# Six VectorE exps per head group instead of five, with the square of their polynomial on GpSimd

## The chip, the cores and the metric

The kernel runs on one core of one Trainium2 chip. A core has TensorE (matrix products, written PE in the profile, its weight loads PEld), VectorE (DVE), ScalarE (ACT), GpSimd (POOL) and SyncE (SP), which here only issues transfers (DMAs). Each engine works through its own queue in order and waits on semaphores for the others. The metric is the device time of one execution in microseconds (us): 11,025.7 us is the median of three runs of the kernel before (11,016.71 to 11,026.11).

## The reference, cut to what matters

The program is a graph network of four layers on 3,327 nodes with 128 features. Nearly all of its time goes to layer 0, an attention with 128 heads of 8 features, in which the adjacency matrix is added to the scores twice:

```python
q = (x @ Wq.T).reshape(d, n, h)          # d = 128 heads, n = 3327, h = 8
k = (x @ Wk.T).reshape(d, n, h)
v = (x @ Wv.T).reshape(d, n, h)
a = jnp.einsum('dnh,dmh->dnm', q, k) * scale
a = a + spatial_encoding + edge_encoding  # both are adj
a = jax.nn.softmax(a, axis=2)
out = jnp.einsum('dnm,dmh->dnh', a, v)
...
return out @ Wo.T
```

So for each of 128 heads a 3,327 x 3,327 matrix of exps is needed. All is fp32.

## The kernel before, in words

**Tiling.** The queries are cut into 7 chunks `c` of 476 columns (`CW`; the last has 472), the heads into 32 groups `g` of four heads `j`, the keys into 13 pairs `q` of two tiles of 128 keys, called even (r = 0) and odd (r = 1). A unit `u` is one (c, g, q): a pair of key tiles for four heads; there are 7 x 32 x 13 = 2,912. A head group is 13 units; there are 224.

**One unit.** PSUM has seven banks `S` for scores and one, `po`, for the sums of values. VectorE seeds a bank with adj minus a bound (`seed`, L641). TensorE adds the scores of head 0, ScalarE takes exp of twice the bank (`exps`, L662 for both banks of a unit in one wide instruction, L665 for one bank where the unit's banks are the first and last of S, which happens to one unit in seven). For heads 1 to 3 TensorE does not start afresh: it adds the scores of head j and subtracts those of head j - 1 in one product (`scores`, L650), as the q tile `QS` holds minus the q of head j - 1 beside the q of head j, and `KT` both heads' keys. The exps of head j of unit u are at slot 4u + 3j of a list of slots `i`, so neighbouring units are interleaved; the seeds, scores and value products (`values`, L705, four heads beside one another) are put between them by the loop over `i` at the end of the function. The order on each engine is the order of the program.

**Exps by hand.** In the units whose q is in `BY_HAND`, the exp of head 0 and the odd tile is made by VectorE: the bank then holds the plain score without seed, VectorE copies it out scaled (L683), seeds the bank for head 1 right behind it, and multiplies up a polynomial of the score in three steps (L687); a last one (L689) multiplies with `EA`, the bare exp of the seed, which is made once per chunk and pair by VectorE (L674) and ScalarE (L675) in `bare`. These steps are a generator, `hand_exp`, of which the slots draw one or two steps at a time. As they end late, `heads_of` lets the value products of the next unit go first. The tile e0 that the result goes into has five buffers.

**Loads.** For the next group `loads` calls, at pair 1, `load_qk`: for each head four transfers of keys into `KT` (16 partitions of 6,656 bytes each, or twice that for heads 1 and 2, where they go to two places) and six or nine small ones of q into `QS` and `QZ`; then one of v. SP issues them; both KT and QS have two buffers by group. At pair 4 GpSimd negates the q of heads 0 to 2 into the place of the next head (`negate_q`, L566, six instructions of 32 partitions), spreads v (L576) and makes a small copy (`all_here`, L580) for which the next group's first score waits. A transfer uses one of eight semaphores in turn, and SP waits for the one before on the same semaphore.

**Other work in the loop.** At the end of a group VectorE copies `po` out (L713) and GpSimd issues four stores (L717), 2.5 pairs into the next group. In about half of the groups 128 rows of adj are partly loaded, turned by VectorE (L288) and searched for row maxima (L292) for a later chunk (class `Square`).

Of the kernel before, what the change touches and what calls it, by code (L numbers as in the profile page):

```python
# [10 lines left out]
F32 = mybir.dt.float32  # L11
# [6 lines left out]
ALU = mybir.AluOpType  # L18
# [70 lines left out]
def gnn_kernel(ctx: ExitStack, tc: tile.TileContext, x, adj, Wq, Wk, Wv, Wo, embed, layer,  # L89
# [435 lines left out]
    with tc.tile_pool(name="e1", bufs=1) as e1, tc.tile_pool(name="e_adj", bufs=28) as e_adj, \  # L525
# [15 lines left out]
        def load_qk(c, g):  # L541

            b = (c * NG + g) % 2
            w, c0 = width_of(c), c * CW
            for j in range(4):
                d = 4 * g + j
                k0, nk = max(0, j - 1), 1 if j in (0, 3) else 2
                q_d = qS_d[:, :, d * N + c0:d * N + c0 + w].rearrange("i e n -> (i e) n")
                for r in range(2):
# [5 lines left out]
                    for q_s in [QS[b][:, j, :]] + [QZ[b]] * ((r, j) == (1, 1)):  # L555
                        nc.sync.dma_start(q_s[r0:r0 + 16, :w].bitcast(F32), q_d)
                        for i in range(2):
                            nc.sync.dma_start(q_s[r0 + 16 + 8 * i:r0 + 24 + 8 * i, :w].bitcast(F32),
                                              q_d[8 - 8 * i:16 - 8 * i])

        def negate_q(c, g):
            b, w = (c * NG + g) % 2, width_of(c)
            for j in range(3):
                for r in range(2):
                    r0 = 64 * r + 32 * (1 - j % 2)
                    nc.gpsimd.tensor_scalar(QS[b][r0:r0 + 32, j + 1, :w], QS[b][r0:r0 + 32, j, :w].bitcast(F32),  # L566
                                            -1.0, 0.0, op0=ALU.mult, op1=ALU.add)
# [27 lines left out]
        with tc.If(loose < 1), tc.manual_schedule():  # L595
# [74 lines left out]

            def bare(c, q):

                w = width_of(c)
                nc.vector.tensor_tensor(EA[q][:, :w], adj_of[c][2 * q + 1][:, :w], shift_of[c][:, :w], op=ALU.subtract)  # L674
                nc.scalar.activation(EA[q][:, :w], EA[q][:, :w], AF.Exp, scale=2.0)  # L675

            def hand_exp(u):
# [11 lines left out]
                nc.vector.scalar_tensor_tensor(e, e, EXP_C[0], EA[pairs[u][2]][:, :w], op0=ALU.add, op1=ALU.mult)  # L689

            def heads_of(u, r):


                first = (u, r)
                if by_hand(u) and r == 1:
                    first = (u + 1, 0)
                elif by_hand(u - 1):
                    first = (u, 1) if r == 0 else (u - 1, 1)
                return [first] + [(u, r)] * 3

            def values(u, r):
                c, g, q = pairs[u]
                w, k = width_of(c), c * NG + g
                for j, (v, of) in enumerate(heads_of(u, r)):
                    nc.tensor.matmul(po[32 * j:32 * j + H + 1, :w], VA[k % 2][:, 2 * pairs[v][2] + of, j, :],  # L705
                                     e_of[v, j][:, 1 - of, :w], start=(q == 0 and r == 0),
                                     stop=(q == NQ - 1 and r == 1))
# [11 lines left out]
            def loads(u):  # L719
# [40 lines left out]
            load_qk(0, 0)  # L760
            shift_of[0] = load_shift(0)
            negate_q(0, 0)
# [728 lines left out]
```

## Time and profile before

| what | value |
|---|---|
| median of the runs | 11,025.7 us |
| the profiled execution, its own time | 11,023.3 us |
| its span, first to last instruction | 11,021.5 us |
| mean granted TensorE clock | 0.985 |
| VectorE's seeds, L641 | 5,824 of 689 ns |
| VectorE's steps, L683, L687, L689 | 5,600 of 650 to 733 ns |
| GpSimd's negations, L566 | 1,344 of 819 ns |
| GpSimd's stores, L717 | 896 of 532 ns |
| transfers into KT | 1,792 of 208 KB and 1,792 of 104 KB |
| transfers into QS and QZ | 6,048 of 15 or 30 KB |

The page gives busy times; an engine's instruction counts as busy from when its waits are over, also while the instruction before it is still running, so that durations can be longer than the pace at which results come. The pace is seen in the timeline, from start to start. "Idle before" is the time in which an engine had nothing under way, with what ended it.

### The profile page before, as it was taken

How to read it: one execution, taken by the hardware profiler on the slowest of the kernel's cores; microseconds unless marked ns; L12 is line 12 of the kernel's file. 1: busy time of each engine (PE TensorE's matmuls, PEld its weight loads, DVE VectorE, ACT ScalarE, POOL GpSimd, SP SyncE). 2: the span in 40 equal slices, each digit the busy share in tenths (PEclk: the TensorE clock that was granted, in tenths of full speed). 3: DMA queues.
4: the chain of work that ended last, by engine and by line, in shares of the span. 5: the costliest groups of instructions: out<-in, count | busy, mean ns of one | idle time of the engine just before them, and what ended most of it. 6: DMA issues, size and time to landing. Idle time of an engine off the chain costs nothing. (4 is left out here: it accounts for less than half of the span.)

```text
span 11021.5 us, 206200 instructions
## 1 busy us (share of the span) xinstructions
PE 10563.2 (96%) x72876; PEld 3424.9 (31%) x72876; DVE 8675.8 (79%) x13503; ACT 10046.2 (91%) x13789; POOL 2177.6 (20%) x3149
## 2 busy tenths in 40 slices
PE   4599999999999999999999999999999999999889
PEld 2123322332223323233332232323323332333544
DVE  5588887888878888788887888878888778887655
ACT  3599999999999999999999999999999999999330
POOL 5122121121112121112122121112112112121101
PEclk7799999999999999999999999999999999999999
DMA  8755555555555554555556555565545545454678
GB/s 248 252 99 96 94 98 108 94 98 96 94 111 98 92 98 85 105 98 98 89 95 119 91 97 91 95 116 97 91 88 97 99 89 88 81 87 72 201 234 281
DMA packets 695348, 1257.08 MB, mean 114 GB/s; under 512 B 195218, under 2 KB 555049, under 8 KB 691244
## 3 DMA queue, kind: packets, MB, share of 16 engines
q1 hardware_dynamic: 644044, 1114.42, 51.0%
q0 software_dynamic: 50272, 129.37, 4.2%
q8 instruction: 590, 9.67, 0.4%
q14 instruction: 442, 3.62, 0.2%
HBM read 1096.53 MB, written 146.60 MB: 113 GB/s over the span
## 5 line engine op out<-in xcount | busy, mean ns | idle before, releaser
L662 ACT ACTIVATE e<-S 128x952 f32<-128x952 f32 (+1 forms) x9024 | 8307.7, 1073 | 40.9 <-PE S L650 27.5
L705 PE MATMUL po<-e,VA 128*9 128x476 f32 (+1 forms) x46592 | 5738.7, 564 | 32.3 <-DVE OS L713 13.0
L641 DVE TENSOR_TENSOR S<-a,shb 128x476 f32<-128x476 f32 (+1 forms) x5824 | 4011.0, 689 | 1337.4 <-ACT e L662 974.5
L650 PE MATMUL S<-QS,KT 64*128 64x476 f32 (+1 forms) x22176 | 4546.8, 444 | 90.2 <-DVE S L641 49.8
L650 PEld LDWEIGHTS S<-QS,KT 64*128 64x128 f32 x22176 | 2083.3, 184 | 5100.3 <-issue 1289.3
L665 ACT ACTIVATE e<-S 128x476 f32<-128x476 f32 (+1 forms) x4128 | 2411.0, 685 | 3.4 <-PE S L650 2.5
L687 DVE SCALAR_TENSOR_TENSOR e<-e,h 128x476 f32<-128x476 f32 (+1 forms) x2240 | 1547.6, 691 | 77.0
L566 POOL TENSOR_SCALAR QS<-QS 32x476 fp32r<-32x476 f32 (+1 forms) x1344 | 1100.3, 819 | 1578.9 <-DMA QS<-qS_d 984.3
L717 POOL DMA_DIRECT2D oT_d<-OS x896 | 472.2, 532 | 4477.1 <-DVE OS L713 4432.9
L705 PEld LDWEIGHTS po<-e,VA 128*9 128x9 f32 x46592 | 691.0, 88 | 1639.8 <-issue 1521.3
L683 DVE TENSOR_SCALAR h<-S 128x476 f32<-128x476 f32 (+1 forms) x1120 | 727.8, 650 | 261.6 <-PE S L650 260.0
L689 DVE SCALAR_TENSOR_TENSOR e<-e,EA 128x476 f32<-128x476 f32 (+1 forms) x1120 | 821.2, 733 | 0.0
L687 DVE SCALAR_TENSOR_TENSOR e<-h 128x476 f32<-128x476 f32 (+1 forms) x1120 | 767.3, 685 | 0.0
L1091 PE MATMUL pu<-strip,y 128*128 128x512 f32 (+2 forms) x1456 | 599.8, 566 | 31.0 <-DVE y L952 14.8
L650 PE MATMUL S<-QZ,KT 64*128 64x476 f32 (+1 forms) x1120 | 487.2, 435 | 11.8 <-DVE S L641 8.1
L576 POOL COPY VA<-VR 128x832 f32<-128x832 f32 x224 | 243.1, 1085 | 985.3 <-DMA VR<-v_d 743.2
L1091 PEld LDWEIGHTS pu<-strip,y 128*128 128x128 f32 (+1 forms) x1456 | 271.6, 191 | 304.7 <-issue 271.9
L1095 DVE TENSOR_REDUCE deg<-strip 128x1 f32<-128x1536 f32 (+1 forms) x104 | 193.8, 1881 | 58.6 <-DMA strip<-adjT 41.9
L650 PEld LDWEIGHTS S<-QZ,KT 64*128 64x128 f32 x1120 | 205.3, 183 | 108.4 <-DVE S L641 60.3
L288 DVE STREAM_TRANSPOSE cols<-rows 128x416 f32<-128x416 f32 x208 | 205.0, 990 | 27.0 <-DMA rows<-in_adj_dram 18.9
L713 DVE COPY OS<-po 128x476 f32<-128x476 f32 (+1 forms) x224 | 146.2, 653 | 97.9 <-PE po L705 97.9
L1044 ACT COPY uT<-pu 128x512 f32<-128x512 f32 (+1 forms) x21 | 11.1, 554 | 222.7 <-PE pu L1091 222.7
(255 smaller groups left out, 1975.8 us busy)
## 6 DMA issues: line engine op xcount, KB each, us to landing
KT<-kS_d SPq DMA_DIRECT2D x1792, 208.0 KB
KT<-kS_d SPq DMA_DIRECT2D x1792, 104.0 KB
VR<-v_d SPq DMA_DIRECT2D x224, 416.0 KB
QS<-qS_d SPq DMA_DIRECT2D x3072, 14.9 KB
QS<-qS_d SPq DMA_DIRECT2D x1536, 29.8 KB
adjT<-cols SPq DMA_DIRECT2D x26, 1664.0 KB
a<-adjT SPq DMA_DIRECT2D x156, 238.0 KB
strip<-adjT POOLq DMA_DIRECT2D x39, 895.5 KB, 5.2
```

The lines of the kernel that those rows point to most:

```text
L566: nc.gpsimd.tensor_scalar(QS[b][r0:r0 + 32, j + 1, :w], QS[b][r0:r0 + 32, j, :w].bitcast(F32), -1.0, 0.0, op0=ALU.mult, op1=ALU.add)
L576: nc.gpsimd.tensor_copy(VA[(c * NG + g) % 2][:, :, :, 0:H], v.rearrange("p j (t e) -> p t j e", e=H))
L641: touch(u, [r], nc.vector.tensor_tensor(bank(u, r), adj_of[c][2 * q + r][:, :w], shift_of[c][:, :w], op=ALU.subtract))
L650: x = nc.tensor.matmul(bank(u, r), KT[b][64 * r:64 * r + 64, max(0, j - 1), q * P:(q + 1) * P], q_s[64 * r:64 * r + 64, :w], start=hand an ...
L662: touch(u, (0, 1), nc.scalar.activation(e[:, :, :w], S[:, odd:even + 1, :w], AF.Exp, scale=2.0))
L665: touch(u, [r], nc.scalar.activation(e[:, 1 - r, :w], bank(u, r), AF.Exp, scale=2.0))
L683: touch(u, [1], nc.vector.tensor_scalar(s, bank(u, 1), EXP_ARG, None, op0=ALU.mult))
L687: nc.vector.scalar_tensor_tensor(e, s if k == 3 else e, EXP_C[k], s, op0=ALU.add, op1=ALU.mult)
L689: nc.vector.scalar_tensor_tensor(e, e, EXP_C[0], EA[pairs[u][2]][:, :w], op0=ALU.add, op1=ALU.mult)
L705: nc.tensor.matmul(po[32 * j:32 * j + H + 1, :w], VA[k % 2][:, 2 * pairs[v][2] + of, j, :], e_of[v, j][:, 1 - of, :w], start=(q == 0 and r ...
L717: nc.gpsimd.dma_start(oT_d[:, d * N + c * CW:d * N + c * CW + w], o[32 * j:32 * j + H + 1, :w])
L1091: nc.tensor.matmul(ps[:, :k], y[:m, t, :], s[:m, c * 4 * P - c0:c * 4 * P - c0 + k], start=(t == 0), stop=(t == NT - 1))
```

## The change

The units with an exp by hand are now at pairs 0, 2, 4, 6, 8 and 10, six per group. The polynomial is rewritten as a product of two quadratics that share one square, plus a constant: VectorE adds a constant to the score (z), GpSimd squares z into e, and VectorE makes three more steps of it, each with two tensors as inputs: four VectorE instructions in place of five. The leading coefficient moves into EA as a shift of its argument. The seed of the bank is still behind the first step. `heads_of` is taken out, and e0 has four buffers. In a chunk's preparation the shift of EA (VectorE) and its exp (ScalarE) are a pair apart.

The loads of the next group are split: at pair 1 all keys, then the q of head 0, then v. At pairs 3, 5 and 7 GpSimd negates one head over all 128 partitions into the next head's place, and SP then loads that head's q over a part of it. The spreading of v and the small copy are at pair 8. On GpSimd's queue each group now has: the square of pair 0, that of pair 2, the four stores, the negation of head 0, the square of pair 4, the negation of head 1, the square of pair 6, the negation of head 2, the square of pair 8, the copies, the square of pair 10.

```diff
-EXP_C = (0.9999990463256836, 2.2162604331970215, 2.4563632011413574, 1.8291265964508057)
-EXP_ARG = 0.9023826718330383
-BY_HAND = (0, 2, 5, 7, 10)
+EXP_C = (0.25674915313720703, 0.05050157010555267, 1.8002841472625732, 0.8117094039916992)
+EXP_LEAD = -0.2054332047700882
+BY_HAND = (0, 2, 4, 6, 8, 10)
...
-        def load_qk(c, g):
+        def load_k(c, g):
...
+        def load_q(c, g, j):
+            b = (c * NG + g) % 2
+            w, c0, d = width_of(c), c * CW, 4 * g + j
+            q_d = qS_d[:, :, d * N + c0:d * N + c0 + w].rearrange("i e n -> (i e) n")
+            for r in range(2):
+                r0 = 64 * r + 32 * (1 - j % 2)
+                for q_s in [QS[b][:, j, :]] + [QZ[b]] * ((r, j) == (1, 1)):
+                    nc.sync.dma_start(q_s[r0:r0 + 16, :w].bitcast(F32), q_d)
+                    for i in range(2):
+                        nc.sync.dma_start(q_s[r0 + 16 + 8 * i:r0 + 24 + 8 * i, :w].bitcast(F32),
+                                          q_d[8 - 8 * i:16 - 8 * i])
+
+        def negate_q(c, g, j):
             b, w = (c * NG + g) % 2, width_of(c)
-            for j in range(3):
-                for r in range(2):
-                    r0 = 64 * r + 32 * (1 - j % 2)
-                    nc.gpsimd.tensor_scalar(QS[b][r0:r0 + 32, j + 1, :w], QS[b][r0:r0 + 32, j, :w].bitcast(F32),
-                                            -1.0, 0.0, op0=ALU.mult, op1=ALU.add)
+            nc.gpsimd.tensor_scalar(QS[b][:, j + 1, :w], QS[b][:, j, :w].bitcast(F32),
+                                    -1.0, 0.0, op0=ALU.mult, op1=ALU.add)
...
-                e = e_of[u, j] = e_e.tile([P, 2, CW], F32, name=f"e{j}", bufs=(5, 4, 3, 2)[j])
+                e = e_of[u, j] = e_e.tile([P, 2, CW], F32, name=f"e{j}", bufs=(4, 4, 3, 2)[j])
...
+            def shifted(c, q):
+                w = width_of(c)
+                nc.vector.scalar_tensor_tensor(EA[q][:, :w], adj_of[c][2 * q + 1][:, :w], EXP_LEAD, shift_of[c][:, :w],
+                                               op0=ALU.add, op1=ALU.subtract)
+
             def bare(c, q):
                 w = width_of(c)
-                nc.vector.tensor_tensor(EA[q][:, :w], adj_of[c][2 * q + 1][:, :w], shift_of[c][:, :w], op=ALU.subtract)
                 nc.scalar.activation(EA[q][:, :w], EA[q][:, :w], AF.Exp, scale=2.0)
 
             def hand_exp(u):
                 w = width_of(pairs[u][0])
-                s = e_h.tile([P, CW], F32, name="h")[:, :w]
+                v, add, mult = nc.vector.scalar_tensor_tensor, ALU.add, ALU.mult
+                z = e_h.tile([P, CW], F32, name="h")[:, :w]
                 e = e_of[u, 0][:, 0, :w]
-                touch(u, [1], nc.vector.tensor_scalar(s, bank(u, 1), EXP_ARG, None, op0=ALU.mult))
+                touch(u, [1], nc.vector.tensor_scalar(z, bank(u, 1), EXP_C[0], None, op0=add))
+                nc.gpsimd.tensor_tensor(e, z, z, op=mult)
                 seed(u, 1)
                 yield
-                for k in (3, 2, 1):
-                    nc.vector.scalar_tensor_tensor(e, s if k == 3 else e, EXP_C[k], s, op0=ALU.add, op1=ALU.mult)
-                    yield
-                nc.vector.scalar_tensor_tensor(e, e, EXP_C[0], EA[pairs[u][2]][:, :w], op0=ALU.add, op1=ALU.mult)
+                v(z, e, EXP_C[1], z, op0=add, op1=add)
+                yield
+                v(e, e, EXP_C[2], z, op0=add, op1=mult)
+                yield
+                v(e, e, EXP_C[3], EA[pairs[u][2]][:, :w], op0=add, op1=mult)
...
                     if q == 1:
-                        load_qk(*nxt)
+                        load_k(*nxt)
+                        load_q(*nxt, 0)
                         v_of[k + 1] = load_v(*nxt)
-                    if q == 4:
-                        negate_q(*nxt)
+                    if q in (3, 5, 7):
+                        negate_q(*nxt, q // 2 - 1)
+                        load_q(*nxt, q // 2)
+                    if q == 8:
                         spread_v(*nxt, v_of.pop(k + 1))
                         here[k + 1] = all_here(*nxt)
...
-                        plan(u - 8 if c else u - 1, bare, c, q)
+                        plan(u - (8 if c else 2), shifted, c, q)
+                        plan(u - (7 if c else 1), bare, c, q)
...
-                for k in range(0 if at % 3 else 1 if at else 0 if by_hand(i // 4) else 2):
+                for k in range(0 if at % 3 or by_hand(i // 4) else 1 if at else 2):
                     if by_vector and next(by_vector[0], True):
                         by_vector.popleft()
```

More of the change, by code (lines that the diff above doesn't have):

```diff
@@ L539, in gnn_kernel @@
         po = e_ps.tile([P, 512], F32, name="po")
-        def load_qk(c, g):
+        def load_k(c, g):
             b = (c * NG + g) % 2
-            w, c0 = width_of(c), c * CW
             for j in range(4):
@@ L547, in load_qk @@
                 k0, nk = max(0, j - 1), 1 if j in (0, 3) else 2
-                q_d = qS_d[:, :, d * N + c0:d * N + c0 + w].rearrange("i e n -> (i e) n")
                 for r in range(2):
@@ L554, in load_qk @@
                                           k_d.unsqueeze(1).to_broadcast([16, nk, NQ * P]))
[L555 to L561, printed above, removed]
-            b, w = (c * NG + g) % 2, width_of(c)
-            for j in range(3):
-                for r in range(2):
-                    r0 = 64 * r + 32 * (1 - j % 2)
-                    nc.gpsimd.tensor_scalar(QS[b][r0:r0 + 32, j + 1, :w], QS[b][r0:r0 + 32, j, :w].bitcast(F32),
-                                            -1.0, 0.0, op0=ALU.mult, op1=ALU.add)
+        def load_q(c, g, j):
[10 more added lines that the diff above has]
+        def negate_q(c, g, j):
+            b, w = (c * NG + g) % 2, width_of(c)
+            nc.gpsimd.tensor_scalar(QS[b][:, j + 1, :w], QS[b][:, j, :w].bitcast(F32),
+                                    -1.0, 0.0, op0=ALU.mult, op1=ALU.add)
         def load_v(c, g):
@@ L680, in hand_exp @@
                 w = width_of(pairs[u][0])
-                s = e_h.tile([P, CW], F32, name="h")[:, :w]
+                v, add, mult = nc.vector.scalar_tensor_tensor, ALU.add, ALU.mult
+                z = e_h.tile([P, CW], F32, name="h")[:, :w]
                 e = e_of[u, 0][:, 0, :w]
-                touch(u, [1], nc.vector.tensor_scalar(s, bank(u, 1), EXP_ARG, None, op0=ALU.mult))
+                touch(u, [1], nc.vector.tensor_scalar(z, bank(u, 1), EXP_C[0], None, op0=add))
+                nc.gpsimd.tensor_tensor(e, z, z, op=mult)
                 seed(u, 1)
                 yield
-                for k in (3, 2, 1):
-                    nc.vector.scalar_tensor_tensor(e, s if k == 3 else e, EXP_C[k], s, op0=ALU.add, op1=ALU.mult)
-                    yield
[L689 to L699, printed above, removed]
+                v(z, e, EXP_C[1], z, op0=add, op1=add)
[3 more added lines that the diff above has]
+                v(e, e, EXP_C[3], EA[pairs[u][2]][:, :w], op0=add, op1=mult)
             def values(u, r):
@@ L703, in values @@
                 w, k = width_of(c), c * NG + g
-                for j, (v, of) in enumerate(heads_of(u, r)):
-                    nc.tensor.matmul(po[32 * j:32 * j + H + 1, :w], VA[k % 2][:, 2 * pairs[v][2] + of, j, :],
-                                     e_of[v, j][:, 1 - of, :w], start=(q == 0 and r == 0),
+                for j in range(4):
+                    nc.tensor.matmul(po[32 * j:32 * j + H + 1, :w], VA[k % 2][:, 2 * q + r, j, :],
+                                     e_of[u, j][:, 1 - r, :w], start=(q == 0 and r == 0),
                                      stop=(q == NQ - 1 and r == 1))
@@ L759, in gnn_kernel @@
             v0 = load_v(0, 0)
-            load_qk(0, 0)
+            load_k(0, 0)
+            load_q(0, 0, 0)
             shift_of[0] = load_shift(0)
-            negate_q(0, 0)
+            for j in range(3):
+                negate_q(0, 0, j)
+                load_q(0, 0, j + 1)
             spread_v(0, 0, v0)
@@ L770, in gnn_kernel @@
                     if u:
-                        plan(u - 8 if c else u - 1, bare, c, q)
+                        plan(u - (8 if c else 2), shifted, c, q)
+                        plan(u - (7 if c else 1), bare, c, q)
+            shifted(0, 0)
             bare(0, 0)
@@ L789, in gnn_kernel @@
                     next(by_vector[-1])
-                for k in range(0 if at % 3 else 1 if at else 0 if by_hand(i // 4) else 2):
+                for k in range(0 if at % 3 or by_hand(i // 4) else 1 if at else 2):
                     if by_vector and next(by_vector[0], True):
                         by_vector.popleft()
-                if at == 0 and i > 0:
+                if at == 0 and i >= 0:
                     for f, a in behind.pop(i // 4, ()):
```

## The prediction

> **What bounds the kernel now.** First the page: shares of the engines, then the groups with the most work.
>
> ```profile
> PE 10563.2 (96%) x72876; PEld 3424.9 (31%) x72876; DVE 8675.8 (79%) x13503; ACT 10046.2 (91%) x13789; POOL 2177.6 (20%) x3149
> ...
> L662 ACT ACTIVATE e<-S 128x952 f32<-128x952 f32 (+1 forms) x9024 | 8307.7, 1073 | 40.9 <-PE S L650 27.5
> ...
> L665 ACT ACTIVATE e<-S 128x476 f32<-128x476 f32 (+1 forms) x4128 | 2411.0, 685 | 3.4 <-PE S L650 2.5
> ```
>
> The attention loop runs from about 560 to 10,210 us, 224 head groups of some 43 us. The windows show that ScalarE is the busiest there (columns: window, length, then PE, PEld, DVE, ACT, POOL busy):
>
> ```profile
> 5000.00:6000.00 1000.00, 992.37 (x7208) 301.35 (x7212) 826.40 (x1244) 996.89 (x1357) 206.41 (x293) 1.00 0.54 96
> ```
>
> A busy 99.7% could still hide waits, so the third view is ScalarE's own timeline (start, length, operation):
>
> ```profile
> 5013.74 8.87 ACT L662 ACTIVATE e<-S 128x952 f32<-128x952 f32 x10
> 5022.31 0.75 ACT L665 ACTIVATE e<-S 128x476 f32<-128x476 f32 x1
> 5022.76 6.30 ACT L662 ACTIVATE e<-S 128x952 f32<-128x952 f32 x7
> ```
>
> From start to start ten wide exps take 8.57 us, 0.857 each, and a single one 0.45. With these paces the 13,152 exps make 9.6 ms, nearly the whole loop: added over the trace, exps end only 0.51 us a group later than their paces allow (115 us in all), 0.19 of it at the first exp of pair 4. ScalarE bounds the loop, and whatever makes it wait is paid in full.
>
> The fourth view is what has slack now and would lose it: GpSimd and the load queue in one group, which starts at 4989.0 (first exp of pair 0).
>
> ```profile
> 4989.69 0.42 SPq L553 DMA_DIRECT2D KT<-kS_d  x1
> ...
> 4999.28 1.68 SPq L553 DMA_DIRECT2D KT<-kS_d  x2
> ...
> 5010.98 0.42 SPq L571 DMA_DIRECT2D VR<-v_d  x1
> ```
>
> ```profile
> 4999.75 1.54 POOL L717 DMA_DIRECT2D oT_d<-OS  x3
> 5001.36 3.61 POOL L566 TENSOR_SCALAR QS<-QS 32x476 fp32r<-32x476 f32 x4
> 5007.42 1.10 POOL L566 TENSOR_SCALAR QS<-QS 32x476 fp32r<-32x476 f32 x1 [2.45 <-PE S L650]
> 5009.80 0.94 POOL L566 TENSOR_SCALAR QS<-QS 32x476 fp32r<-32x476 f32 x1 [1.27 <-DMA QS<-qS_d]
> 5014.50 1.39 POOL L576 COPY VA<-VR 128x832 f32<-128x832 f32 x1 [3.77 <-DMA VR<-v_d]
> ```
>
> SP needs over 20 us to issue a group's loads, since each waits for the eighth before it to land. GpSimd stores at 10 us into the group, starts negating at 12.3, waits for loads, and ends at 26; nobody needs that before the next group.
>
> **The change, part by part.**
>
> *Exps.* A sixth exp per group leaves ScalarE. One pair in seven has its two banks at the ends of S and uses singles already. So of 224 exps 192 turn a wide one into a single, and 32 drop a single: wide 9024 to 8832, single 4128 to 4288. That is -192 x 0.857 + 160 x 0.45 = -164.5 + 72 = **-92 us**. VectorE's steps fall from 25 to 24 a group (about 0.69 each by the L687 row); VectorE isn't the bound, so that is worth nothing.
>
> *Values.* TensorE's matmuls stay the same in number; those of a hand pair take its own exps again (heads_of goes), 13 ScalarE slots after the pair's start, while the last step is done within 8. With four e0 buffers instead of five a buffer is written again at slot 16; two slots, 1.7 us, cover that. Nothing; it would cost the lateness if the steps came five slots late.
>
> *Bare exps.* The wait below goes, as the shift is now one pair earlier, and seven bare exps at 0.60 come: **-23 us**.
>
> ```profile
> ACT EA L675 <- DVE EA L674: 26.9, 26, 1.7
> ```
>
> *Squares on GpSimd.* Its nearest rows are the products in the first stage:
>
> ```profile
> L369 POOL TENSOR_TENSOR sq<-sq 128x512 f32<-128x512 f32 x52 | 66.0, 1270 | 28.5 <-ACT sq L367 27.3
> L369 POOL TENSOR_TENSOR sq<-sq 128x256 f32<-128x256 f32 x52 | 37.6, 723 | 4.2
> ```
>
> 547 ns for 256 elements give 1.19 us at 476. GpSimd and VectorE block each other: one negation alone takes 0.58; a two-input VectorE instruction that starts inside it ends 0.51 after GpSimd's end, and GpSimd behind VectorE ends 0.44 after VectorE's end, 0.15 less than alone. One-input instructions (L683, 0.65 either way) don't care. A row inside the four negations at 5001.36:
>
> ```profile
> 5002.83 1.03 DVE L689 SCALAR_TENSOR_TENSOR e<-e,EA 128x476 f32<-128x476 f32 x1
> ```
>
> Beside no GpSimd work L689 takes 0.65. Now the hand exp: z ends at 0; the seed of its own bank starts 0.035 later and ends at 0.695; the square ends 1.04 after that, 1.74; the next pair's seed, ready at 1.1 to 1.3 and done at 1.7 to 2.0 today, ends at 1.74 + 0.51 = 2.25. From a seed's end to its exp's start pass 0.57 us where ScalarE waits for it (pair 4), and 0.77 to 0.92 behind hand pairs: 0.2 to 0.35 us of slack. So 0 to 0.15 us is lost per hand pair; I take 0.07 for five of them (pair 4 is below): 5 x 0.07 x 224 = **+80 us**, with 0 and +170 as ends. VectorE's second step needs e about 3 us after z, which 1.74 satisfies.
>
> The Trainium skill ("SBUF — State Buffer", "Who interferes with whom") says the loser blocks for the whole instruction. By it the seed would end at 0.695 + 1.19 + 0.66 = 2.55, and this part would be some 340 us more (an estimate); the rows above show a start-up that overlaps.
>
> *Negations.* Three of 128 partitions in place of six of 32: the time goes by the 476 columns, 0.58 alone. The 0.19 us a group lost at pair 4 lies just behind today's row of negations; it goes, or is swallowed by what follows: **-43 us**. At the start three rounds of load and negation follow one another: **+8 us**.
>
> *The order of loads, where I expect the damage.* Before, head 0's q came behind two K transfers. Now all 16 K transfers (2.5 MB) come first, then six of q for head 0; the first negation waits for those; and on GpSimd's in-order queue stand: square of pair 2, four stores, negation 0, **square of pair 4**. Behind that square VectorE waits with its second step, and behind it the seeds and z of pair 6.
>
> When does q land? From the landings in the trace (16 semaphore updates each): a first 104 KB transfer takes 2.5 us; following ones of 104 KB come 0.35 to 0.6 apart, those of 208 KB 0.5 to 1.8 apart. In the quarter of groups that load earliest, eight of 208 KB and the 15 small ones between them land within 16.8 us; with 0.35 for a small one that is 1.44 each, and 1.33 without the first. I take 1.3, 0.5 and 0.35: 2.5 + 3 x 0.5 + 8 x 1.3 + 4 x 0.5 + 6 x 0.35 = 18.5 us from the first issue. Ends: 0.9 and 0.4 (14.6 us), 1.5 and 0.55 (20.5).
>
> The skill's same page ("Door 1: The DMA port swizzle") gives 104 GB/s for 16 partitions: 2 us for 208 KB, so 26 us in all and about 1,700 us more than my sum (an estimate). The landings above are faster than that where several transfers overlap.
>
> First issue, from the group's start, in 220 groups: -1.7 in 126 (held by PE's use of the buffer; about 0.8 more is lost waiting for its later parts), 0.0 in 64 (rows of adj are loaded first), 2.5 in 8 (chunk's last group), 7.0 in 22 (SP waits there for the row maxima to come back). So q lands at 17.6, 18.5, 21 and 25.5.
>
> When is it needed? Pair 4 starts after two hand pairs (0.45 + 3 x 0.857 = 3.03, with one split in seven 3.06) and two others (3.46): 13.04. z ends 0.35 later, the step follows 3.05 later: 16.45. The square is done 0.1 + 0.65 + 1.2 = 2 us after q lands. VectorE thus waits landing - 14.45; z and the seed of pair 6 have 0.6 of slack before ScalarE runs dry. Loss: 2.55, 3.45, 6 and 10.45 us: 126 x 2.55 + 64 x 3.45 + 8 x 6 + 22 x 10.45 = 820, scaled to 224 groups **+835 us**. The next two negations wait too, each for q loads that SP may issue only after the negation before, but by the same reckoning they are done at about 25 and 30, within a us of the need; I count nothing more. The copies of V and of K's first column move behind the square of pair 8, to some 32 us; their cover is the rest of the group, 10 us.
>
> Sum: -92 - 23 + 80 - 43 + 8 + 835 = +765. The profiled execution took 11,023.3 us (span 11,021.5), 2 below the median 11,025.7: **11,790 us**.
>
> **Rivals.**
>
> *Only the late groups wait* (0.10). K streams at 0.9: landing 13.7, 14.6, 17, 21.6; loss 0, 0, 2, 6.6, so 160 us; with -70 from the rest 11,110. For it: pairs of K transfers at times land 0.2 to 0.5 apart. Against: over whole groups they don't.
>
> *Faster* (0.07): K lands at 0.5 each, seeds lose nothing to squares, and only 22 groups still wait 2.6 us: -150 + 58, 10,930 us. It decides once q lands before 14.5 us. Against it: in this trace K's 2.5 MB and what lies between take over 20 us in every group.
>
> *The port costs more* (0.12): the square holds VectorE for all its length, +0.35 at five pairs: 390 more, 12,180.
>
> **How the numbers follow.** The main case has 0.68, the rest (0.03) is no change. Its ends are 90 and 1,200 us above: 11,115 to 12,225; taking in the first rival, 11,100 to 12,250. What a measurement tells from no change is 0.2%, 22 us: faster 0.07, same 0.03, slower 0.90.
>
> **What would show it.** Right: VectorE's second step idle behind GpSimd for 2 to 4 us once a group, GpSimd's first negation behind the q load for 5 us or more, ScalarE down to some 93% in the loop, group period near 46 us. Wrong: the first negation starting at 12 to 14 us, or waits spread over all six hand pairs (then it is the port).

## The result, and the profile after

The changed kernel takes 13,090.4 us (median of four runs, 13,082.4 to 13,091.1) against 11,023.4 us for the kernel before on the same chip: a ratio of 1.187, interval 1.186 to 1.189. The forecast was 11,790 us with a range up to 12,250. The direction and the place of the loss were as forecast, its size was not: +2,067 us where +765 had been added up.

The page of the changed kernel, with the rows that answer to those shown of the kernel before:

```profile
PE 10979.2 (84%) x72876; PEld 3471.3 (27%) x72876; DVE 8625.7 (66%) x13286; ACT 10020.5 (77%) x13764; POOL 3294.5 (25%) x3821
...
PE 42%; DMA 34%; DVE 11%; POOL 3%; ACT 3%; issue 2%; SPq 1%; POOLq 0%; DVEq 0%; ACTq 0%
DMA KT<-kS_d 29%; PE po L707 21%; PE S L654 16%; DMA QS<-qS_d 5%; DVE S L645 5%; PE pu L1101 4%; ACT e L666 2%; DVE h L693 2%; POOL e L694 2%; DVE h L697 2%; DVE e L699 1%; POOL QS L570 1%; SPq L551 1%; DVE cols L288 1%; ACT e L669 0%
...
L666 ACT ACTIVATE e<-S 128x952 f32<-128x952 f32 (+1 forms) x8832 | 8209.7, 1064 | 1810.2 <-PE S L654 1803.0
...
L697 DVE SCALAR_TENSOR_TENSOR h<-e,h 128x476 f32<-128x476 f32 (+1 forms) x1344 | 869.6, 647 | 1897.5 <-POOL e L694 1897.5
...
L570 POOL TENSOR_SCALAR QS<-QS 128x476 fp32r<-128x476 f32 (+1 forms) x672 | 425.9, 634 | 3616.9 <-DMA QS<-qS_d 3571.9
```

ScalarE does about as much as before (10,020.5 us against 10,046.2) in a span that is 2,059 us longer. The second line is the chain of what ended last: transfers hold 34% of it, where they held 1% in the kernel before. The wide exps (L666) now have 1,810 us of idle time before them. The two rows below are the links behind them: VectorE's second step (L697) idle for 1,897.5 us behind GpSimd's square (L694), GpSimd's negations (L570) idle for 3,572 us behind the loads of q. The list of waits has how many times (total, times, longest):

```profile
POOL QS L570 <- DMA QS<-qS_d: 3571.9, 658, 29.3
...
DVE h L697 <- POOL e L694: 1897.5, 227, 17.1
ACT e L666 <- PE S L654: 1803.0, 640, 15.8
```

The middle row has 227 waits in 224 groups of six steps each: one wait a group, 8.4 us on average. The timeline of one group whose pair 0 starts at 5237 shows which:

```profile
5259.42 0.58 POOL L570 TENSOR_SCALAR QS<-QS 128x476 fp32r<-128x476 f32 x1 [9.34 <-DMA QS<-qS_d]
5259.98 0.97 POOL L694 TENSOR_TENSOR e<-h 128x476 f32<-128x476 f32 x1
...
5260.98 0.66 DVE L697 SCALAR_TENSOR_TENSOR h<-e,h 128x476 f32<-128x476 f32 x1 [7.05 <-POOL e L694]
...
5264.77 0.76 PE L654 MATMUL S<-QZ,KT 64*128 64x476 f32 x1 [5.88 <-DVE S L645]
...
5265.46 1.78 PE L707 MATMUL po<-e,VA 128*9 128x476 f32 x8
5265.57 0.96 ACT L666 ACTIVATE e<-S 128x952 f32<-128x952 f32 x1 [5.60 <-PE S L654]
...
5268.00 0.96 ACT L666 ACTIVATE e<-S 128x952 f32<-128x952 f32 x1 [1.47 <-PE S L654]
...
5270.83 0.99 PE L707 MATMUL po<-e,VA 128*9 128x476 f32 x8
```

GpSimd had stood idle for 9.34 us, until q of head 0 was there for the first negation; the square of pair 4 starts 0.56 us behind it, VectorE's step after the square, then the seed of pair 6, TensorE's score of head 1, and the exp. That is the chain that the prediction drew, at its place. What it did not have is the rest: the next exp waits another 1.47 us, and eight value products take 1.78 us at 5265.46 and 0.99 us at 5270.83. From 5263.68 to 5270.51 TensorE's granted clock was half of full speed. Over the trace there are 244 such stretches of half clock, 2,347 us in all; 223 of them (2,014 us) are those of the stalls and set in while the stall lasts; most of the others lie outside the loop.

I also added up, over the exps in order, how much later each ends than ScalarE's pace allows (0.857 us for a wide one, 0.46 for a single one): the excess. It is 0.51 us per group before and 10.09 after: 7.07 at one exp, head 1 of pair 6, 2.36 at two exps behind it, head 0 of pair 7 and head 2 of pair 6 (whose slot is among those of pair 7, so that both count as pair 7 below), and 0.66 everywhere else. A group takes 52.74 us (mean) where it took 43.52; times 223 that is +2,056 us, the whole loss.

### The profile page after: what moved, and what is told of

Read it like the earlier page. It is cut to its first block, busy times and chain, and to the rows that moved or that the text cites. A ratio compares the mean times of both kernels' runs of the same rounds, so it can differ in the third digit from the quotient of the medians.

```text
span 13080.6 us, 205819 instructions
## 1 busy us (share of the span) xinstructions
PE 10979.2 (84%) x72876; PEld 3471.3 (27%) x72876; DVE 8625.7 (66%) x13286; ACT 10020.5 (77%) x13764; POOL 3294.5 (25%) x3821
## 3 DMA queue, kind: packets, MB, share of 16 engines
q1 hardware_dynamic: 644044, 1114.42, 47.8%
## 4 chain that ended last, share of the span: by engine, by line
PE 42%; DMA 34%; DVE 11%; POOL 3%; ACT 3%; issue 2%; SPq 1%; POOLq 0%; DVEq 0%; ACTq 0%
DMA KT<-kS_d 29%; PE po L707 21%; PE S L654 16%; DMA QS<-qS_d 5%; DVE S L645 5%; PE pu L1101 4%; ACT e L666 2%; DVE h L693 2%; POOL e L694 2%; DVE h L697 2%; DVE e L699 1%; POOL QS L570 1%; SPq L551 1%; DVE cols L288 1%; ACT e L669 0%
## 5 line engine op out<-in xcount | busy, mean ns | idle before, releaser
L666 ACT ACTIVATE e<-S 128x952 f32<-128x952 f32 (+1 forms) x8832 | 8209.7, 1064 | 1810.2 <-PE S L654 1803.0
L707 PE MATMUL po<-e,VA 128*9 128x476 f32 (+1 forms) x46592 | 6059.5, 594 | 28.2
L645 DVE TENSOR_TENSOR S<-a,shb 128x476 f32<-128x476 f32 (+1 forms) x5824 | 4340.8, 745 | 1566.1 <-ACT e L666 1172.2
L694 POOL TENSOR_TENSOR e<-h 128x476 f32<-128x476 f32 (+1 forms) x1344 | 1756.3, 1307 | 4769.6 <-DVE h L693 3290.6
L669 ACT ACTIVATE e<-S 128x476 f32<-128x476 f32 (+1 forms) x4288 | 2509.8, 681 | 295.1 <-PE S L654 293.7
L697 DVE SCALAR_TENSOR_TENSOR h<-e,h 128x476 f32<-128x476 f32 (+1 forms) x1344 | 869.6, 647 | 1897.5 <-POOL e L694 1897.5
L654 PE MATMUL S<-QZ,KT 64*128 64x476 f32 (+1 forms) x1344 | 673.5, 501 | 1703.1 <-DVE S L645 1703.1
L570 POOL TENSOR_SCALAR QS<-QS 128x476 fp32r<-128x476 f32 (+1 forms) x672 | 425.9, 634 | 3616.9 <-DMA QS<-qS_d 3571.9
L693 DVE TENSOR_SCALAR h<-S 128x476 f32<-128x476 f32 (+1 forms) x1344 | 873.4, 650 | 316.3 <-PE S L654 308.4
L699 DVE SCALAR_TENSOR_TENSOR e<-e,h 128x476 f32<-128x476 f32 (+1 forms) x1344 | 878.2, 653 | 46.1
L701 DVE SCALAR_TENSOR_TENSOR e<-e,EA 128x476 f32<-128x476 f32 (+1 forms) x1344 | 868.8, 646 | 0.0
```

The source lines that it names most:

```text
L570: nc.gpsimd.tensor_scalar(QS[b][:, j + 1, :w], QS[b][:, j, :w].bitcast(F32), -1.0, 0.0, op0=ALU.mult, op1=ALU.add)
L645: touch(u, [r], nc.vector.tensor_tensor(bank(u, r), adj_of[c][2 * q + r][:, :w], shift_of[c][:, :w], op=ALU.subtract))
L654: x = nc.tensor.matmul(bank(u, r), KT[b][64 * r:64 * r + 64, max(0, j - 1), q * P:(q + 1) * P], q_s[64 * r:64 * r + 64, :w], start=hand an ...
L666: touch(u, (0, 1), nc.scalar.activation(e[:, :, :w], S[:, odd:even + 1, :w], AF.Exp, scale=2.0))
L669: touch(u, [r], nc.scalar.activation(e[:, 1 - r, :w], bank(u, r), AF.Exp, scale=2.0))
L693: touch(u, [1], nc.vector.tensor_scalar(z, bank(u, 1), EXP_C[0], None, op0=add))
```

## The experiments

Three theories. **Q**: the squares stand behind the negations in GpSimd's in-order queue, and these wait for q. **L**: the time goes with the new order of loads as such, whoever waits for it. **P**: GpSimd's squares hold VectorE's seeds back (the shared port of the prediction). All runs were compared with the kernel before on the same chip; edits are against the changed kernel unless another is named.

**Out of the queue: the square made by VectorE.**

```diff
-                nc.gpsimd.tensor_tensor(e, z, z, op=mult)
+                nc.vector.tensor_tensor(e, z, z, op=mult)
```

> The changed kernel with the square made by VectorE; the new order of loads and negations stays. Theory Q (GpSimd's in-order queue: the square of pair 4 stands behind a negation that waits for q): VectorE no longer waits for GpSimd, the 7 us idle time before its second step is gone, 10,950 to 11,200 us (30 hand instructions a group instead of 25 make VectorE fuller). Theory L (the new order of loads is late for TensorE itself): still about 13,000. Theory P (squares and VectorE's two-input instructions block each other): also back to about 11,000, so this run does not tell Q from P.

11,487.6 us, ratio 1.042 (1.040 to 1.043). L falls: loads and negations are the changed kernel's, and 1,600 of the 2,067 us are gone. It is above Q's 10,950 to 11,200, and the excess tells where: 0.2 to 0.6 us at the first exp of every pair that follows a hand pair, some 2.5 us of the 2.97 per group. The list of waits has it as many short ones:

```profile
ACT e L666 <- PE S L654: 396.2, 1111, 7.8
```

1,111 waits against 640: an instruction of 0.67 us between z and the seed makes the seed late by some 0.45 us. So there is about 0.2 us of slack on the seeds, the lower end of the 0.2 to 0.35 of the prediction. With the square on GpSimd the same exps show an excess of 0.00 to 0.05 in pairs 1 to 5: the port that the prediction priced at 80 us costs nothing there.

**Later negations: pairs 5, 7, 9 and pairs 7, 9, 11** (in place of 3, 5, 7).

> Only the pairs change at which a negation and the q load behind it are issued: 5, 7, 9 instead of 3, 5, 7. The square of pair 4 is then ahead of the first negation. Theory Q: the first negation still starts at some 22 us, now in front of the square of pair 6, whose result is needed at 23: at most a us lost in most groups, 8 to 10 us in the 22 groups whose loads start late; 11,100 to 11,400 us. Theories L and P: nothing changes, about 13,000.

> The same with pairs 7, 9, 11: q has landed in all but the late groups before the first negation is reached. Theory Q: no wait for GpSimd, 10,880 to 11,000 us, faster than the kernel before, by the exp, the bare exps and fewer waits at pair 4, less what the squares cost the seeds. Theories L and P: about 13,000.

11,317.0 us, ratio 1.027 (1.025 to 1.028), and 11,014.6 us, ratio 0.999 (0.998 to 1.000). With nothing but the place of three instructions in the program (and the q loads tied to them) the loss goes by 86% and then wholly. The first lies in Q's range; the second is 15 us above it and no faster than the kernel before within 0.2%. There the steps still wait now and then:

```profile
DVE h L697 <- POOL e L694: 126.3, 59, 4.3
```

**The old order of loads, the old six negations, at pair 4, with the new exps.**

```diff
-                        load_k(*nxt)
-                        load_q(*nxt, 0)
+                        load_qk(*nxt)
...
-                    if q in (3, 5, 7):
-                        negate_q(*nxt, q // 2 - 1)
-                        load_q(*nxt, q // 2)
-                    if q == 8:
+                    if q == 4:
+                        negate_q(*nxt)
                         spread_v(*nxt, v_of.pop(k + 1))
...
```

> The changed kernel with loads and negations as before: q behind its head's keys, six negations and both copies at pair 4. Theory Q: undoing the order of loads does not help, as the squares of pairs 6 and 8 now stand behind the six negations and the copy of v, which end at 26 to 29 us; the wait moves to pair 6 and 8, 5 to 8 us a group, 12,200 to 12,900 us. Theory L: the loads are as before, so about 11,000. Theory P: about 13,000.

12,675.4 us, ratio 1.149 (1.147 to 1.151). Restoring the loads doesn't help; Q is hit. The wait is the same, in this kernel's line numbers:

```profile
DVE h L693 <- POOL e L690: 1517.9, 223, 16.7
```

It now sits at the square of pair 6 (excess 5.09 at head 1 of pair 8). The kernel before had this very row of negations, loads and copies: it was free only as long as nothing urgent stood behind it on GpSimd.

**How early q must be: behind 12 of the 16 K transfers, and ahead of all.**

```diff
...
-                        load_k(*nxt)
+                        load_k(*nxt, range(3))
                         load_q(*nxt, 0)
+                        load_k(*nxt, range(3, 4))
```

> The changed kernel with one edit: the q of head 0 is loaded behind the K transfers of heads 0 to 2, so that the four 104 KB transfers of head 3 come after it. By theory Q with the measured 0.65 us for each of these, the q lands 4 x 0.65 = 2.6 us earlier in each of 224 groups, and the time falls by 2.6 x 224 = 580 us, to about 12,500 us, somewhat lower if the slow stretch of TensorE after the stall grows shorter too. Theory L: about 13,090 us.

12,565.3 us, ratio 1.140 (1.138 to 1.142): 525 us less for four transfers of 104 KB, 2.34 us per group of the 2.6 expected. L falls again; the landing of this one q sets the time almost one for one.

```diff
-                        load_k(*nxt)
                         load_q(*nxt, 0)
+                        load_k(*nxt)
```

> The changed kernel with one edit: the q of head 0 is loaded ahead of the sixteen K transfers, not behind them. Theory Q (the first negation, in GpSimd's queue ahead of the square of pair 4, waits for the q that lands behind the K transfers): the first negation no longer waits and pair 4's step runs on time; but the q of head 1 is still issued behind the K transfers, lands some 23 us into the group, and the second negation (pair 5) then holds the square of pair 6 for some 2 us: 11,500 to 11,700 us. Theory L (the time goes with the transfers as such, whoever waits for them): nothing but the place of one small transfer has changed, so about 13,000 us.

11,798.0 us, ratio 1.070 (1.068 to 1.072). The stall of pair 6 is gone, and the second negation makes one at pair 8 (excess 2.40, and 1.16 in pair 9), as Q says; the time is 100 us above its range, since I had counted the stall without what follows it, and nothing for pair 5 (see the run with pairs 3, 7 and 9).

**K transfers over 32 partitions instead of 16.**

```diff
-                    for i in range(2):
-                        nc.sync.dma_start(KT[b][r0 + 16 * i:r0 + 16 * i + 16, k0:k0 + nk, :].bitcast(F32),
-                                          k_d.unsqueeze(1).to_broadcast([16, nk, NQ * P]))
+                    for k in range(k0, k0 + nk):
+                        nc.sync.dma_start(KT[b][r0:r0 + 32, k, :].bitcast(F32),
+                                          k_d.unsqueeze(0).to_broadcast([2, 16, NQ * P]))
```

> The changed kernel with the K transfers shaped differently: each goes to 32 partitions and one plane (208 KB) where it went to 16 partitions and two planes (208 KB) or one (104 KB); the bytes are the same, in 12 transfers instead of 16. If what limits a transfer is the number of partitions that it writes, the last K lands some 7 us into its sequence instead of 14, the q of head 0 some 6 us earlier, and the stall nearly goes: 11,100 to 11,500 us. If it is the bytes alone (one stream's rate, whatever the partitions), q lands as now: 13,000 to 13,150 us.

20,070 us, ratio 1.820 (1.817 to 1.823): both readings missed. A transfer of 208 KB lands 4.1 us after the one before it (median), where it takes 1.70 in the changed kernel. The queue's row of the page (packets, MB, time that they took as a share of 16 engines) for this run, and then for the changed kernel:

```profile
q1 hardware_dynamic: 592076, 1114.22, 18.1%
```

```profile
q1 hardware_dynamic: 644044, 1114.42, 47.8%
```

18.1% of 20,087 us is 3,640, 47.8% of 13,081 is 6,250: the same bytes kept the 16 engines less busy and still landed later. Few engines at work per transfer would look like this. The Trainium skill ("DMA: Bandwidth & Descriptors", "Why a DMA increments its semaphore by 16 and not by 1") says that a transfer is spread over the largest number up to 16 that divides the outermost dimension of both sides; the source of this run begins with a dimension of 2. Two engines at the 27.2 GB/s per port of "SBUF — State Buffer" ("Door 1: The DMA port swizzle") are 54 GB/s, an estimate; the 208 KB in 4.1 us are 52. The trace doesn't name the engines of a transfer, but the updates of its semaphore fit two: each of the 2,688 K transfers of this run has three, one right behind its issue and two at the landing, where each of the 3,584 of the changed kernel has 16. The run therefore says nothing on the question that it was made for, what 32 partitions are worth.

**Is the second loss the clock?** 30 small matmuls ahead of the score that waits:

```diff
+                            if (pairs[u][2], j) == (6, 1):
+                                for m in range(30):
+                                    nc.tensor.matmul(po[:, 480:512], EA[0][:, :P], EA[0][:, :32], start=True, stop=True,
+                                                     skip_group_check=True)
                             scores(u, j)
```

> The changed kernel with 30 small matmuls (128x128 by 32 columns, into columns of the accumulator's bank that nothing reads) ahead of the score matmuls of head 1 of pair 6, so that TensorE works for part of the stall instead of standing still for all of it. In the changed kernel its granted clock is 0.5 in a stretch of 7 to 10 us behind each stall, and ScalarE loses 2.4 us per group there (pairs 7 and 8) above the stall itself. If the slow clock makes these 2.4 us, and TensorE's idle time brings the slow clock on, the clock stays up and most of 2.4 x 224 = 540 us goes: 200 to 500 us under 13,090 us, 12,590 to 12,890 us. If the loss in pairs 7 and 8 is only the refill of the pipeline (VectorE's late seeds), the time stays at 13,050 to 13,200 us.

13,503.3 us, ratio 1.225 (1.223 to 1.227). The added products also spoil the result; only the time is read. Neither number: 410 us more. TensorE in one group:

```profile
5966.94 10.12 PE L819 MATMUL po<-EA 128*128 128x32 f32 x60
...
5977.69 1.77 PE L707 MATMUL po<-e,VA 128*9 128x476 f32 x8
...
5980.47 0.99 PE L707 MATMUL po<-e,VA 128*9 128x476 f32 x8
```

It never idled, and its clock fell all the same: the added products start 0.11 us apart until 5970.1, 0.21 from there, so they last 10 us, and the wait at this exp grows from 7.07 to 9.21 us per group. Pair 7 loses 2.14 us, little less than before. The run says that such small products don't hold the clock, and nothing on what a full clock would be worth.

That can be read from groups that a run has anyway. In the run with negations in pairs 5, 7, 9, 19 groups stall for 1.0 to 1.5 us at pair 8. In 5 of them no value product behind the stall is slow, and pair 9 loses 0.58 us on average; in the other 14 it loses 1.83. Two of them in windows of 8 us from the delayed exp on (columns: window, length, busy time of PE, PEld, DVE, ACT, POOL, granted clock, DMA share, GB/s), the first after a stall of 1.13 us, the second of 1.18:

```profile
2993.60:3001.60 8.00, 8.00 (x53) 2.12 (x56) 6.98 (x10) 6.30 (x8) 3.84 (x5) 0.79 0.13 29
5233.40:5241.40 8.00, 7.53 (x57) 2.05 (x56) 7.72 (x10) 7.45 (x9) 4.25 (x5) 1.00 0.16 30
```

At equal stalls the clock of 0.79 costs ScalarE 1.15 us of work in the window (6.30 against 7.45). Behind stalls of that length the slow clock is thus worth 1.25 us (1.83 less 0.58), and a refill of some 0.5 us is left at full clock. In the changed kernel 216 of 223 stalls are over 4 us, and all are followed by half clock; the seven short ones (0.6 to 3.6 us) lose 2.1 to 3.0 us in pair 7 all the same. What full clock is worth at the same place is seen in the run with q behind 12 transfers: five of its groups stall for 1.7 to 2.2 us at pair 6 with no half clock in the 5 us behind the late exp, and these lose 0.5 us in pair 7, where its groups lose 2.15 on average. Of the 2.36 us some 1.9 are thus the clock's.

**A version that beats both?** Five placements, of which each but the last showed the next wait.

```diff
-                        load_k(*nxt)
                         load_q(*nxt, 0)
+                        load_k(*nxt)
...
-                    if q in (3, 5, 7):
+                    if q in (3, 7, 9):
...
-                    if q == 8:
+                    if q == 11:
```

> The changed kernel with the q of head 0 loaded first, the three negations in pairs 3, 7 and 9 instead of 3, 5 and 7, and the copies of V and K in pair 11 instead of 8: each negation stands where its q has landed. Theory Q: no step waits for GpSimd, so that only ScalarE's own pace and the start remain: 10,900 to 10,980 us, 0.4 to 1% faster than the kernel before. Theory P (GpSimd's squares block VectorE's port and so its seeds, whoever waits for loads): no faster than the kernel before, 11,020 us or more.

11,179.8 us, ratio 1.014 (1.012 to 1.016): neither. Of 222 groups 194 have next to no stall at pair 10; 22 lose 2.8 to 4.8 us there and one 7.5, behind the second q. There is another loss, 0.39 us per group (87 us in all) at the first exp of pair 5, as in the run with q first; it is 0.05 in the changed kernel. The first negation now runs beside the last of VectorE's steps for pair 2 (L701), which takes 1.17 us (median) where it takes 0.65 in the changed kernel, and z of pair 4 behind it is late: a delay of P's kind, at one place.

The old loads with six negations, these behind the square of pair 8 (`if q == 8`), the copies behind that of pair 10 (`if q == 10`):

> The new exps, with the loads in the order of the kernel before, the six negations of 32 partitions behind the square of pair 8 in GpSimd's queue, and the copies of V and K behind that of pair 10: the last q has landed 25.6 us into the group (median), pair 8's square is done some 28 us into it, and pair 10's comes 6.5 us later. Theory Q: no square waits for a load but in the latest groups, so that the terms of the prediction other than the 835 us remain: 10,880 to 10,990 us, 0.3 to 1.3% faster than the kernel before. Theory P (GpSimd's work holds VectorE's seeds back whatever it waits for): 11,020 us or more, with excess of ScalarE in pairs 8 to 12.

11,065.4 us, ratio 1.004 (1.002 to 1.005). The list of waits has no row any more for steps behind squares; the excess is 0.33 at pair 10 and 0.55 at pair 11, the latter in all groups alike. P's reading is the nearer here: work on GpSimd at a hand pair would delay a seed. The next run fits that, with next to no excess at either place once the copies have left pair 10, but it moves the negations too.

Negations in pairs 8, 10, 12, copies in pair 11, loads as in the changed kernel:

```diff
-                    if q in (3, 5, 7):
-                        negate_q(*nxt, q // 2 - 1)
-                        load_q(*nxt, q // 2)
-                    if q == 8:
+                    if q in (8, 10, 12):
+                        negate_q(*nxt, q // 2 - 4)
+                        load_q(*nxt, q // 2 - 3)
+                    if q == 11:
```

> The changed kernel with its three negations moved from pairs 3, 5 and 7 to 8, 10 and 12, where each stands behind the square of its own pair in GpSimd's queue and has two pairs' time before the next square, and the copies of V and K in pair 11 instead of 8. Theory Q (squares wait for loads through GpSimd's order): even the latest groups have their q before the next square, the excess of ScalarE that the run with 7, 9 and 11 has in pairs 10 to 12 (0.56 us per group, 125 us in all) goes: 10,880 to 10,960 us. Theory P (what is left there is GpSimd's copies and negations holding back VectorE's seeds, wherever they stand): it moves to the pairs where the copies stand now, 10,980 to 11,070 us.

11,037.8 us, ratio 1.001 (1.000 to 1.002): in P's range, but not for P's reason. Pairs 1 to 12 have 0.2 us of excess; 0.73 is at the first exps of pair 0, and it comes from 22 groups that wait for several us (of the 26 stores that the recorded texts count, four lie ahead of the loop). The timeline of one:

```profile
4132.30 0.54 SPq L295 DMA_DIRECT2D adjT<-cols  x1
4133.11 0.81 POOL L570 TENSOR_SCALAR QS<-QS 128x476 fp32r<-128x476 f32 x1 [5.21 <-DMA QS<-qS_d]
...
4133.95 8.24 SPq L562 DMA_DIRECT2D QS<-qS_d  x1
...
4146.24 0.58 POOL L570 TENSOR_SCALAR QS<-QS 128x476 fp32r<-128x476 f32 x1 [11.38 <-DMA QS<-qS_d]
4146.77 0.87 POOL L580 COPY VA<-VR 128x832 f32<-128x832 f32 x1
...
4147.83 1.44 PE L654 MATMUL S<-QS,KT 64*128 64x476 f32 x4 [5.98 <-POOL seen L584]
```

The q for the second negation is issued behind a store of 1,664 KB of a turned square of adj (L295); the negation waits until 4146.2, the copies behind it, and the next group's first score behind the copies.

The same run with the store on ScalarE's queue, and the read of the maxima in pair 6 (`(6, sq.back), (9, sq.finish)`):

> The run with the negations in pairs 8, 10 and 12 and two edits more, for its 26 late groups (those of a square of the adjacency being turned; there the first exps of the next group wait 0.73 us per group on average, since the second negation waits until some 46 us into the group for a q that is behind a store of 1,664 KB in SP's queue, and the copies of V and K wait behind it): the store goes to ScalarE's DMA queue, and the read of the square's maxima, which holds the K loads back by some 8 us in these groups, is issued in pair 6 instead of 1 (its use in pair 9 instead of 7). Theory Q (queue order is all that is left): the excess of 0.73 us at the first pair goes, 0.73 x 224 = 160 us less than 11,038: 10,860 to 10,930 us, about 1% faster than the kernel before. Theory P (GpSimd's work as such holds the seeds): no change, 11,000 to 11,050 us.

11,132.1 us, ratio 1.010 (1.008 to 1.011). The wait at pair 0 is gone (excess 0.00), but in the same groups the K transfers now come late: in one of them SP issues none between 17.4 and 35.3 us of the group. The read of the maxima goes out behind them at 39, and VectorE waits for it, 226.9 us in 22 groups, with an excess of 0.92 at pair 10. The wait moved, and the trace shows what holds K: the store takes its turn on one of the eight semaphores, and the next K transfer is the one that uses this semaphore after it. In all 22 groups SP issues it 0.02 us after the store has landed, 33.0 to 35.3 us into the group.

The run with pairs 8, 10 and 12 again, the store left on SP's queue and issued five pairs later, at pair 0 of the next group, behind the last q (the recorded texts call this a group later):

```diff
-                    for k, f in ((0, sq.gather), (1, sq.back), (7, sq.finish), (8, sq.store)):
+                    for k, f in ((0, sq.gather), (1, sq.back), (7, sq.finish), (13, sq.store)):
```

> The run with the negations in pairs 8, 10 and 12 and one edit: the store of 1,664 KB of a turned square, in 26 groups, is issued a group later, behind all of the group's q loads in SP's queue, where it stood ahead of the second q. Theory Q (queue order is all that is left): the second negation no longer waits for a q behind that store, the 0.73 us per group at the first pair go (160 us), and the K loads of the next group, now behind the store, give back some 1 to 2 us in each of 26 groups (25 to 50 us): 10,890 to 10,960 us, faster than the kernel before by 0.6 to 1.2%, as the sum of the prediction without its 835 us has it (10,956 us). Theory P (GpSimd's work as such holds the seeds): no change, 11,000 to 11,050 us.

**10,901.3 us, ratio 0.989 (0.987 to 0.991)**, in Q's range, faster than both kernels. Its page:

```profile
PE 10462.4 (96%) x72876; PEld 3438.3 (32%) x72876; DVE 8642.5 (79%) x13286; ACT 9930.3 (91%) x13764; POOL 3515.4 (32%) x3821
...
L666 ACT ACTIVATE e<-S 128x952 f32<-128x952 f32 (+1 forms) x8832 | 8241.4, 1105 | 38.6 <-PE S L654 36.5
...
L697 DVE SCALAR_TENSOR_TENSOR h<-e,h 128x476 f32<-128x476 f32 (+1 forms) x1344 | 989.7, 736 | 10.1 <-POOL e L694 10.1
```

ScalarE bounds again, with 38.6 us of idle time before the wide exps, and the steps wait 10.1 us in all for 1,344 squares.

Last, the same move of the store in the kernel before:

> The kernel before with the one edit of the last run: the store of a turned square a group later. If the six exps as such made the last run faster (its 1.1%), the kernel before, whose squares of the pairs wait for no load, gains little or nothing from the edit: 10,980 to 11,050 us. If the store's place made it, the kernel before gains about as much: 10,880 to 10,930 us.

11,022.5 us, ratio 1.000 (0.999 to 1.001): the store alone is worth nothing there. So the 1.1% come with the rest of the change, the six exps with their squares on GpSimd, once nothing in GpSimd's queue waits ahead of a square. At ScalarE's paces the new counts of exps are worth 92 us; 0.2 us less excess per group than in the kernel before are another 46. The new loads with the old five exps were not run.

## Why the prediction was wrong, point by point

- **The mechanism** (negation 0 waits for q, the square of pair 4 behind it, VectorE's step, the seed of pair 6, the exp) was right in every link, and the runs with another queue order, another engine for the square and a q that lands earlier show it.
- **The step that failed is the sizing of the 835 us: the rate of the K transfers.** I took 1.3 us for 208 KB and 0.5 for 104 KB, so 18.5 us from the first issue to q. The landings in the trace are 1.70 and 0.65 apart, and q lands 23.2 us after the first issue in the groups that load earliest: 21.5, 23.4, 24.4 and 29.3 us into the group for the four kinds, where I had 17.6, 18.5, 21 and 25.5. Put into the prediction's own formula (landing less 14.45 less 0.6), these give 1,770 us; the stall at pair 6 measured 7.07 x 224 = 1,584. The 1.3 came from one sum in the kernel before, eight K transfers and 15 small ones in 16.8 us, by taking off 0.35 for each small one, for which no row was given, and leaving out the first K. In the changed kernel the six small ones behind the last K land within 1.26 us of it, 0.21 each; eight times 1.70 and 15 times 0.21 make 16.8 us as well. So K may have taken 1.70 in the kernel before too, and the split of the sum hid it; or K overlapped more with the small ones between them, as landings of two K with none between them, 1.3 to 1.8 apart there, suggest. No run tells these apart. The Trainium skill ("SBUF — State Buffer", "Door 1: The DMA port swizzle") gives 104 GB/s for 16 partitions; the trace has 213 KB in 1.70 us, 125 GB/s. I had set this rule aside for the overlapping rows; the measured rate lies nearer to it than to mine, and the 26 us that it gave are 3 above the 23.2, my 18.5 are 4.7 below.
- **A term was left out: what follows the stall.** Pair 7 loses 2.36 us per group, 530 us, by TensorE at half clock (some 1.9 us) and the refill (some 0.5 us). The prediction counted a stall as if the engines went on at their pace behind it.
- **Squares on GpSimd, +80:** about 0 in the changed kernel. The square starts 0.15 us after z and takes 1.38 us beside a seed, 0.97 alone (estimate: 1.19), and no step of the pairs without a negation ahead waits for it. Where GpSimd's work falls beside VectorE's steps just ahead of z, as in the run with pairs 3, 7 and 9, it does cost: 87 us at one place.
- **Exps and bare exps, -92 and -23, wait at pair 4, -43, start, +8:** not to be read from the changed kernel, where the stall covers them. In the version that beats both nothing does: a group takes 42.91 us (mean) against 43.52, times 223 that is -136 us, and the time is 124 less, where these terms without the +80 make -150. As a sum they are right to some 25 us; of the single terms only the wait at pair 4 is seen by itself, 0.19 us a group before and 0.01 in that version.
- **The negations after the first** "within a us of the need": in the changed kernel they start at 27.5 and 31.8 us and cause no further stall, as the first one has moved the need as well. In the run with q first the second one is the stall.
- **The signs to look for:** the step's wait is 8.4 us a group instead of 2 to 4, ScalarE is at 82.5% in the window from 5,000 to 6,000 us instead of 93%, a group takes 52.7 us instead of 46.
- **The rivals:** that only late groups wait and that it is faster had needed K at 0.9 us and less; K came at 1.70. "The port costs more" had waits spread over all hand pairs; there is one wait a group.

As a sum, from the measured parts and the prediction's own terms for the exps: -115 (exps and bare exps) + 1,584 (stall) + 530 (behind it) + 34 (0.66 less 0.51 us elsewhere) = 2,033 us of the 2,059 between the spans.

## What to carry to other kernels

Putting an instruction that is needed within 3 us on an engine's in-order queue makes everything ahead of it in that queue urgent, also what waited there for a load at no cost before: look at what stands ahead of it, by when its data lands, not only at its duration. Take a transfer's rate from a row of transfers of the same kind back to back, not from a mix; and count a stall with what comes after it, here a third on top.

## What the runs showed of the hardware

- **Equal stalls, unequal clocks.** In the changed kernel TensorE's granted clock falls to 0.5 within the stall, 4.3 us ahead of the late exp, and stays there for 10.2 us (medians). With stalls of 1.0 to 1.5 us in the run with pairs 5, 7 and 9 it falls in 14 groups of 19 only, for 3.4 us in 13 of them. Of the changed kernel's 244 stretches of half clock all but one last a whole multiple of 3.41 us. The Trainium skill ("TensorE: Matmul & The Clock Gate", Part 1) has a free-running activity window of about 3.4 us as the cause, which fits the multiples and a fall that depends on when a stall comes; that an idle stretch of 1.5 us can be enough (1.48 in the group above whose clock fell, 1.57 in the one whose clock did not) is less than the page's window.
- **Busy isn't enough.** A row of matmuls of 128x128 by 32 columns, 0.11 us apart without a gap, lost the full clock after 3.2 us in the group shown, and 2.4 to 5.8 us after its start in 218 of the run's 224 groups.
- **Two shares instead of sixteen.** A K transfer of 208 KB to 32 partitions, from a source with an outer dimension of 2, has three semaphore updates and lands 4.1 us after the one before it (52 GB/s); to 16 partitions, with 16, it has 16 updates and lands after 1.70 us (125 GB/s). Both sides of the transfer were changed at once, so that the outer dimension alone does it is not shown.
- **One semaphore for two queues.** A K transfer on SP's queue waited for a store of 1,664 KB on ScalarE's queue that had the same semaphore: issued 0.02 us after the store's landing, 22 times of 22.
- **A square of one tensor** on GpSimd (both inputs the same) takes 0.97 us for 128x476 alone and 1.38 when a seed of VectorE starts just ahead of it.
